# q at the edges for two quads at once, in row groups beside the first layers, in a graph attention kernel

## The chip, the core and the metric

The kernel runs on one core of a Trainium2 chip, as one launch. The metric is the device time in microseconds. The kernel before was timed in three runs, and one more execution was recorded by the hardware profiler; all stage times below are from that recorded execution.

## The reference

There are 6250 nodes with 128 features each and 206250 directed edges from a sender (`src`) to a receiver (`dst`), sorted by receiver. Cut to what matters:

```python
w   = silu(edge_feats @ rad_W1 + rad_b1) @ rad_W2 + rad_b2
w  += silu(chi_scalar @ sph_W1 + sph_b1) @ sph_W2 + sph_b2        # per edge, 32 -> 128 -> 128
q_i = (x @ Wq)[receivers];  k_j = (x @ Wk)[senders];  v_j = (x @ Wv)[senders]
alpha = (q_i * w * k_j) summed over the 16 features of each of 8 heads, / sqrt(16), * cutoffs
out = segment_sum(alpha * v_j, receivers) / 16
return layernorm(x + out)
```

All arithmetic is float32.

## The kernel before, in words

**Stages.** First the node stage: x is loaded in 13 chunks, turned on TensorE, multiplied with Wk and Wv, and the 256-wide rows of k and v are stored to a table `kv_tab` in HBM (lines 195 to 230). For the first 8 quads k and v are made directly from gathered rows of x. Then comes the edge stage, which fills nearly the whole time.

**Tiling of the edges.** 128 edges are a tile, 4 tiles are a quad (512 edges), 4 quads are a group (2048 edges): 101 groups, 403 quads. A quad's 512 edges belong to at most 32 consecutive receivers, a group's to at most 128. The edges are sorted by receiver, so q at the edges needs no gather: it is a matmul of the quad's 32 rows of q with a one-hot matrix (`hotT`, 32 x 512). The sender's k and v do need one: `gathers` (line 132) has GpSimd issue 4 indirect DMAs for each quad, 128 rows of 1 KB each, all recorded under line 114. They go to a ring of 16 quad buffers and are issued 14 quads ahead in the program.

**One quad.** `weigh` (line 382) multiplies the two hidden layers (`act`) with the second-layer weights into PSUM, and ScalarE brings it out as `w` (line 388). `take_q` (line 391) makes q at the edges in PSUM (`pq`, line 395), with features on partitions; VectorE multiplies both to `u` (line 399). `turn_back` (line 401) turns `u` with four TensorE transposes so that edges lie on partitions (`pu`, line 405). VectorE multiplies with k (`m`, line 410), sums by head (412), scales (413) and multiplies with v (`msg`, line 421). `sum_quads` (line 425) adds messages to receivers by a one-hot matmul (line 431), a group later.

**First layers.** `hidden` (line 363) makes the four first layers of a pair of quads: each has 32 contraction rows, so the four lie in the four 32-row groups of TensorE (line 372, PSUM tiles `ph`, 4 buffers, shared with `weigh` and small products), and ScalarE applies Silu (line 378). A quad j of a group has its q rows in row group j.

**Order.** The order of all engines is written out by hand. Quads are taken in slots 0 to 3 in the order j = 0, 2, 1, 3. Each slot of TensorE is: `weigh` of this quad, `turn_back` of the quad before, `take_q` of this quad, in slots 0 and 2 `hidden` for the next pair; then small products of the group: in slot 1 `sum_group` (453, 455) and `turn_q` (341), in slot 3 `make_q` (349), and parts of `sum_quads`. VectorE does `scores` of the quad before, `multiply` of this quad, `messages` of the quad before. Each gather is given a wait for a TensorE instruction of its own slot (`marks`).

**Queue of SyncE (SP).** In slot 0 it issues `load_q` (line 158): four loads, each of 32 rows of x at a row read from a table (line 119 the read, 163 the load), for the next group's `turn_q` in slot 1; then `load_xw` (128 rows of x for the layernorm) and `load_rel` (four loads that spread the edges' receiver offsets over 32 partitions each). Slot 1 has the edge features. After every fourth group `statistics` (line 464) has ScalarE change its function table, normalise four groups, and SP stores four blocks of `out` (line 486).

Of the kernel before, what the change touches and what calls it, by code (L numbers as in the profile page):

```python
# [2 lines left out]

# [18 lines left out]
WAIT = mybir.DependencyInfo(mybir.DependencyClass.Sync, mybir.DependencyReason.DATA)  # L22
# [30 lines left out]
def gnn_kernel(ctx, tc, x, src, dst, weight, edges, rad_W1, rad_b1, rad_W2, rad_b2,  # L53
# [38 lines left out]
    qb_i = const.tile([1, NG * NQ], I32, name="qb_i")  # L92
    gb_i = const.tile([1, NG], I32, name="gb_i")
    rowq = const.tile([P, NG], F32, name="rowq")
# [18 lines left out]
    def gather(o, table, index):  # L113
        return nc.gpsimd.indirect_dma_start(  # L114
            out=o, out_offset=None, in_=table,
            in_offset=bass.IndirectOffsetOnAxis(ap=index, axis=0))
# [14 lines left out]
    feats_of, relb_of, act_of, kv_of, hot_of, hotT_of, xq_of, q_of, msg_of = ({} for _ in range(9))  # L131
    po_of, part_of, to_of, tot_of, xw_of, y0_of, u_of = ({} for _ in range(7))

    def gathers(q, marks=()):

        kv = quad_of("kv", RING, 2 * D)
        for t in range(QT):
            o = gather(kv[:, t, :], kv_tab, src_i[:, q * QT + t:q * QT + t + 1])
            if marks:
                tc.add_manual_dep(o.ins, marks[t].ins.name, WAIT, reason="no gather ahead of TensorE")  # L140
        kv_of[q] = kv
# [8 lines left out]
    def load_rel(g):  # L150

        relb_of[g] = gp.tile([P, EQ], BF16, name="relb")
        for j in range(NQ):
            t = g * GT + j * QT
            nc.sync.dma_start(relb_of[g][j * W:(j + 1) * W, :],
                              rel_lin[t:t + QT, :].rearrange("t e -> (t e)").partition_broadcast(W))

    def load_q(g):

        xq_of[g] = gp.tile([P, D], F32, name="xq")  # L160
        for j in range(quads_in(g)):
            r = start_of(qb_i, g * NQ + j, N - W)
            nc.sync.dma_start(xq_of[g][j * W:(j + 1) * W, :], x[ds(r, W), :])  # L163
# [18 lines left out]
    with tc.tile_pool(name="nodes", bufs=1) as nodes, \  # L182
# [3 lines left out]
        xs_of, xT_of = {}, {}  # L186
# [7 lines left out]
        def load_x(k):  # L194
# [62 lines left out]
        def tables():  # L257
            nc.vector.tensor_scalar(gb, qb[:, :, 0], float(N - P), None, op0=OP.min)
            nc.vector.tensor_copy(qb_i, qb[:1].rearrange("p g j -> p (g j)"))
            nc.vector.tensor_copy(gb_i, gb[:1])  # L260
            load_q(0)
# [4 lines left out]
            nc.vector.tensor_scalar(rowq, rowq, roww, None, op0=OP.add)  # L266
            nc.vector.tensor_copy(rowwp, roww)
            nc.vector.tensor_copy(colp, col)
# [34 lines left out]
        for k in range(8):  # L303
            load_x(k)
            if k == 5:
                nc.sync.dma_start(dst_i, dst)
# [3 lines left out]
        for i, (k, n) in enumerate(work):  # L310
            if i + 2 < len(work):
                turn(*work[i + 2])
            kvs = k_and_v(k, n)
            for o, w in smalls[i:i + 1]:
                nc.scalar.dma_start(o, w)
            if i >= len(chunks):
                kv_of[k[0]] = kvs
                continue
            store(k, kvs)
            if k + 8 < len(chunks):  # L320
                load_x(k + 8)
# [15 lines left out]
    with tc.tile_pool(name="ps", bufs=1, space=PSUM) as pp:  # L337
        def turn_q(g):
            n = quads_in(g) * W
            pt = pp.tile([P, EQ], F32, name="ph", bufs=4)  # L340
            nc.tensor.transpose(pt[:, :n], xq_of[g][:n, :], ident[:n, :n])  # L341
            xq_of[g] = gp.tile([P, P], F32, name="xqT")
            nc.scalar.activation(xq_of[g][:, :n], pt[:, :n], AF.Copy)

        def make_q(g):

            n = quads_in(g) * W
            pt = pp.tile([P, EQ], F32, name="ph", bufs=4)
            nc.tensor.matmul(pt[:n, :D], xq_of[g][:, :n], wq, start=True, stop=True)  # L349
            q_of[g] = gp.tile([P, D], F32, name="q")  # L350
            nc.scalar.activation(q_of[g][:n, :], pt[:n, :D], AF.Copy)  # L351
# [12 lines left out]
        def hidden(pair):  # L364

            for q in pair:
                g, j = divmod(q, NQ)
                r0, c0 = 2 * R * (j // 2), EQ * (j % 2)
                for i in range(2):
                    ph = pp.tile([P, EQ], F32, name="ph", bufs=4)  # L370
                    r = slice(r0 + i * R, r0 + (i + 1) * R)
                    o = nc.tensor.matmul(ph, w1[r, :], feats_of[g][r, c0:c0 + EQ],  # L372
                                         start=True, stop=True)
                    act_of[q, i] = ph
            for q in pair:
                for i in range(2):
                    act = ep.tile([P, EQ], F32, name="act", bufs=8)
                    nc.scalar.activation(act, act_of[q, i], AF.Silu, bias=b1[:, i:i + 1])  # L378
                    act_of[q, i] = act
            return o  # L380

        def weigh(q):

            pw = pp.tile([P, EQ], F32, name="ph", bufs=4)
            for i in range(2):
                o = nc.tensor.matmul(pw, w2[:, i, :], act_of[q, i], start=(i == 0), stop=(i == 1))  # L386
            w = ep.tile([P, EQ], F32, name="w")
            nc.scalar.activation(w, pw, AF.Identity, bias=bsum)  # L388
            return w, o

        def take_q(q):
            g, j = divmod(q, NQ)
            b = slice(j * W, (j + 1) * W)
            pq = pp.tile([P, EQ], F32, name="pq")
            return pq, nc.tensor.matmul(pq, q_of[g][b, :], hotT_of[g][b, :], start=True, stop=True)  # L395

        def multiply(q, pq, w):
            u_of[q] = ep.tile([P, EQ], F32, name="u")
            nc.vector.tensor_tensor(u_of[q], pq, w, op=OP.mult)  # L399

        def turn_back(q):

            pu = pp.tile([P, QT, D], F32, name="pu")
            for t in range(QT):
                o = nc.tensor.transpose(pu[:, t, :], u_of[q][:, t * P:(t + 1) * P], ident)  # L405
            return pu, o
# [19 lines left out]
        def sum_quads(g, t, j=None):  # L426
# [3 lines left out]
            for j in range(NQ) if j is None else (j,):  # L430
                o = nc.tensor.matmul(po_of[g][j * W:(j + 1) * W, :], hot_of[g][:, j * QT + t, :],  # L431
                                     msg_of[g * NQ + j][:, t, :], start=(t == 0), stop=(t == QT - 1))
            return o
# [25 lines left out]
        def load_xw(g):  # L459
            r = start_of(gb_i, g, N - P)  # L460
            xw_of[g] = gp.tile([P, D], F32, name="xw")
            nc.sync.dma_start(xw_of[g], x[ds(r, P), :])

        def statistics(g):
# [5 lines left out]
            nc.vector.tensor_tensor(y0[:, k - 1, :], tot_of[g], xw_of[g], op=OP.add)  # L470
# [39 lines left out]

        turn_q(0)
# [5 lines left out]
        hidden(pairs[0])  # L517
        before = None
        for g in range(NG):
            last = g == NG - 1  # L520
            for slot, j in enumerate((0, 2, 1, 3)):
                q = g * NQ + j
                i = g * NQ + slot
                if q >= QUADS:
                    continue
                if slot == 0 and 2 <= g:
# [18 lines left out]
                if 1 <= g:  # L545
                    for t in ((), (0, 1), (2, 3))[slot] if last else ((), (0, 1), (2,), (3,))[slot]:
                        marks[3] = sum_quads(g - 1, t)
# [4 lines left out]
                multiply(q, pq, w)  # L552
# [3 lines left out]
                if slot == 0:  # L556
                    if g + 1 < NG:
                        load_q(g + 1)
                    if 1 <= g:
                        load_xw(g - 1)  # L560
                        if g + 1 < NG:
                            load_rel(g + 1)
                if slot == 1:
# [4 lines left out]
                    if last:  # L568
                        place(g)
                        load_xw(g)  # L570
# [9 lines left out]
        pu, _ = turn_back(before)  # L580
# [169 lines left out]
```

## Time and profile before

| what | us |
|---|---|
| median of 3 runs | 2080.5 (2072.03 to 2083.07) |
| profiled execution, own time | 2093.36 |
| its span, first to last instruction | 2091.3 |
| TensorE matmuls busy | 1919.3 |
| GpSimd busy | 1526.5 |
| VectorE busy | 1411.4 |
| ScalarE busy | 1000.9 |
| mean granted TensorE clock | 0.967 |

"Busy" is the union of an engine's instructions. Every float32 matmul of 512 columns is recorded as two passes; a busy TensorE is therefore not one at its peak. A group's row in the profile gives line, engine, operation, output<-inputs and count, then busy time and the mean duration in ns, then the idle time of the engine ahead of it and what ended that idle time ("issue": nothing that the profile shows). In the chain of work the columns are start, length and what. The granted clock is a share of full speed.

### The profile page before, as it was taken

What the parts mean: (1) busy time and instruction counts of PE and PEld (TensorE: products, weight loads), DVE (VectorE), ACT (ScalarE), POOL (GpSimd) and SP (SyncE); (2) the same over time, 40 slices, a digit from 0 to 9 for tenths busy, and PEclk for the clock granted to TensorE, in tenths of its full rate; (3) what the DMA queues carried; (4) which work ended last, traced back from release to release, by engine and by line L of the source; (5) the groups of instructions that cost most, each with busy time, mean ns of one, the idle gap of its engine ahead of it and who ended that gap; (6) DMA issues with size and microseconds to landing.
All of it is one profiled execution on the core that took longest, in us unless ns stands there. A gap on an engine that the chain in (4) does not pass through costs nothing.

```text
span 2091.3 us, 33176 instructions
## 1 busy us (share of the span) xinstructions
PE 1919.3 (92%) x9843; PEld 920.2 (44%) x9843; DVE 1411.4 (67%) x2874; ACT 1000.9 (48%) x1826; POOL 1526.5 (73%) x1620
## 2 busy tenths in 40 slices
PE   8998999989999989988998989899989999899897
PEld 7444444444444434444444444444444444444443
DVE  6676766767766766766766767667667667667666
ACT  2444545544544445444445445445445444454453
POOL 6777777777777777777777777777777777777750
PEclk9999999999999999999999999999999999999998
DMA  8545455454454454445544554554554544544540
GB/s 300 156 151 153 139 154 154 138 155 145 147 157 145 146 148 151 150 146 149 153 144 143 152 152 139 155 155 139 153 149 143 157 144 146 157 144 147 149 123 14
DMA packets 166853, 310.49 MB, mean 148 GB/s; under 512 B 46530, under 2 KB 99212, under 8 KB 166668
## 3 DMA queue, kind: packets, MB, share of 16 engines
q0 software_dynamic: 76864, 209.29, 34.3%
q1 hardware_dynamic: 88316, 98.64, 14.5%
q8 instruction: 79, 1.29, 0.2%
q14 instruction: 106, 0.87, 0.1%
q10 hardware_dynamic: 1488, 0.40, 0.1%
HBM read 294.70 MB, written 13.46 MB: 147 GB/s over the span
## 4 chain that ended last, share of the span: by engine, by line
PE 76%; ACT 9%; DMA 5%; issue 3%; SPq 3%; DVE 2%; POOL 1%; ACTq 0%; DVEq 0%
PE ph L386 32%; PE pq L395 14%; PE ph L372 11%; PE pu L405 8%; PE po L431 6%; ACT act L378 6%; DMA out<-y 2%; DMA xq<-in_x 2%; PE ph L453 2%; PE ph L349 2%; POOL msg L114 1%; SPq L163 1%; ACT y L483 1%; SPq L119 1%; PE ph L341 1%
## 5 line engine op out<-in xcount | busy, mean ns | idle before, releaser
L114 POOL DMA_INDIRECT kv<-kv_tab,src_i x1580 | 1494.8, 946 | 486.2 <-issue 261.4
L386 PE MATMUL ph<-act,w 128*128 128x512 f32 x1612 | 837.0, 644 | 78.6 <-ACT act L378 78.6
L410 DVE TENSOR_TENSOR m<-pu,kv 128x512 f32<-128x512 f32 x403 | 278.6, 691 | 557.6 <-PE pu L405 554.4
L378 ACT ACTIVATE act<-ph,b 128x512 f32<-128x512 f32 x806 | 498.5, 686 | 252.8 <-PE ph L372 239.9
L388 ACT ACTIVATE w<-ph,bsum 128x512 f32<-128x512 f32 x403 | 276.5, 686 | 456.9 <-PE ph L386 455.3
L386 PEld LDWEIGHTS ph<-act,w 128*128 128x128 f32 x1612 | 285.1, 197 | 432.4 <-issue 248.1
L395 PE MATMUL pq<-hotT,q 32*128 32x512 f32 x806 | 452.8, 641 | 0.0
L372 PE MATMUL ph<-feats,w 32*128 32x512 f32 x1612 | 398.5, 629 | 0.0
L405 PEld LDWEIGHTS pu<-ident,u 128*128 128x128 f32 x1612 | 204.1, 144 | 242.2 <-issue 155.6
L399 DVE TENSOR_TENSOR u<-pq,w 128x512 f32<-128x512 f32 x403 | 274.6, 681 | 23.7 <-ACT w L388 14.3
L412 DVE TENSOR_REDUCE side<-m 128x32 f32<-128x512 f32 x403 | 280.1, 695 | 13.7
L421 DVE TENSOR_TENSOR msg<-kv,side 128x512 f32<-128x512 f32 x403 | 272.8, 677 | 0.0
L405 PE MATMUL pu<-ident,u 128*128 128x128 f32 x1612 | 247.4, 277 | 12.7 <-DVE u L399 12.7
L372 PEld LDWEIGHTS ph<-feats,w 32*128 32x128 f32 x1612 | 158.2, 185 | 73.1 <-issue 56.1
L431 PE MATMUL po<-msg,hot 128*32 128x128 f32 x3224 | 161.4, 295 | 2.9 <-ACT part L448 2.9
L395 PEld LDWEIGHTS pq<-hotT,q 32*128 32x128 f32 x806 | 118.6, 184 | 69.7 <-issue 69.7
L431 PEld LDWEIGHTS po<-msg,hot 128*32 128x32 f32 x3224 | 75.8, 113 | 108.8 <-issue 91.3
L457 ACT ACTIVATE tot<-ph 128x128 f32<-128x128 f32 x101 | 28.0, 277 | 148.2 <-PE ph L455 139.8
L413 DVE TENSOR_TENSOR side<-side,scale 128x32 f32<-128x32 f32 x403 | 80.4, 200 | 13.8
L341 PE MATMUL ph<-ident,xq 128*128 128x128 f32 (+1 forms) x101 | 30.1, 298 | 60.8 <-DMA xq<-in_x 60.4
L351 ACT ACTIVATE q<-ph 128x128 f32<-128x128 f32 (+1 forms) x101 | 27.5, 272 | 93.1 <-PE ph L349 88.2
L360 DVE TENSOR_TENSOR hot<-rel,side 128x512 f32<-128x512 f32 x101 | 68.7, 681 | 0.0
(83 smaller groups left out, 837.2 us busy)
## 6 DMA issues: line engine op xcount, KB each, us to landing
feats<-in_edges SPq DMA_DIRECT2D x101, 512.0 KB
kv<-kv_tab,src_i POOLq DMA_INDIRECT x1580
relb<-rel_lin SPq DMA_DIRECT2D x404, 32.0 KB
xw<-in_x SPq DMA_DIRECT2D x101, 64.0 KB
out<-y SPq DMA_DIRECT2D x101, 64.0 KB
xq<-in_x SPq DMA_DIRECT2D x403, 16.0 KB
kv_tab<-kv SPq DMA_DIRECT2D x12, 512.0 KB
act<-in_x SPq DMA_DIRECT2D x12, 256.0 KB
```

What stands on the lines that cost most here:

```text
L114: return nc.gpsimd.indirect_dma_start(out=o, out_offset=None, in_=table, in_offset=bass.IndirectOffsetOnAxis(ap=index, axis=0))
L372: o = nc.tensor.matmul(ph, w1[r, :], feats_of[g][r, c0:c0 + EQ], start=True, stop=True)
L378: nc.scalar.activation(act, act_of[q, i], AF.Silu, bias=b1[:, i:i + 1])
L386: o = nc.tensor.matmul(pw, w2[:, i, :], act_of[q, i], start=(i == 0), stop=(i == 1))
L388: nc.scalar.activation(w, pw, AF.Identity, bias=bsum)
L395: return pq, nc.tensor.matmul(pq, q_of[g][b, :], hotT_of[g][b, :], start=True, stop=True)
L399: nc.vector.tensor_tensor(u_of[q], pq, w, op=OP.mult)
L405: o = nc.tensor.transpose(pu[:, t, :], u_of[q][:, t * P:(t + 1) * P], ident)
L410: nc.vector.tensor_tensor(m, pu, kv_of[q][:, :, :D], op=OP.mult)
L412: nc.vector.tensor_reduce(alpha, m.rearrange("p t (h e) -> p t h e", e=HD), AX.X, OP.add)
L421: nc.vector.tensor_tensor(msg_of[q].rearrange("p t (h e) -> p t h e", e=HD), kv_of[q][:, :, D:].rearrange("p t (h e) -> p t h e", e=HD), a ...
L431: o = nc.tensor.matmul(po_of[g][j * W:(j + 1) * W, :], hot_of[g][:, j * QT + t, :], msg_of[g * NQ + j][:, t, :], start=(t == 0), stop=(t = ...
```

## The change

**q at the edges for a pair at once.** `take_q` and `hidden` become `q_and_hidden`. In slots 0 and 2 it makes q at the edges for both quads of the present pair, and the four first layers of the next pair: the two q products use two row groups (0 and 2, or 1 and 3), the first two first layers the other two, and the last two first layers come after.

**PSUM.** `pq` and `pu`, which had one bank each, become one tile name with two banks, in turn.

**Order of TensorE.** `turn_back` of the quad before now stands ahead of `weigh` of this quad. Slots 1 and 3 have no q product any more.

**Rows of x.** `load_q` and `load_xw` become one `load_x` of the group's 128 rows, issued two groups ahead, 6 buffers. The 32-row windows of the quads are picked out of it by a matmul with a one-hot matrix `pick`, made by VectorE once a group, where a transpose stood. `off` for it is made in the node stage. `load_rel` is one load instead of four.

**Gathers.** The waits for TensorE (`marks`) go, and the issue of a slot's gathers stands at the top of the slot.

```diff
-    qb_i = const.tile([1, NG * NQ], I32, name="qb_i")
+    off = const.tile([P, NG, NQ], F32, name="off")
...
-    def gathers(q, marks=()):
+    def gathers(q):
         kv = quad_of("kv", RING, 2 * D)
         for t in range(QT):
-            o = gather(kv[:, t, :], kv_tab, src_i[:, q * QT + t:q * QT + t + 1])
-            if marks:
-                tc.add_manual_dep(o.ins, marks[t].ins.name, WAIT, reason="no gather ahead of TensorE")
+            gather(kv[:, t, :], kv_tab, src_i[:, q * QT + t:q * QT + t + 1])
...
         relb_of[g] = gp.tile([P, EQ], BF16, name="relb")
-        for j in range(NQ):
-            t = g * GT + j * QT
-            nc.sync.dma_start(relb_of[g][j * W:(j + 1) * W, :],
-                              rel_lin[t:t + QT, :].rearrange("t e -> (t e)").partition_broadcast(W))
-
-    def load_q(g):
-        xq_of[g] = gp.tile([P, D], F32, name="xq")
-        for j in range(quads_in(g)):
-            r = start_of(qb_i, g * NQ + j, N - W)
-            nc.sync.dma_start(xq_of[g][j * W:(j + 1) * W, :], x[ds(r, W), :])
+        r = rel_lin[g * GT:(g + 1) * GT, :].rearrange("(j t) e -> j (t e)", j=NQ)
+        nc.sync.dma_start(relb_of[g], r[:, None, :].to_broadcast([NQ, W, EQ]))
+
+    def load_x(g):
+        r = start_of(gb_i, g, N - P)
+        x_of[g] = gp.tile([P, D], F32, name="x", bufs=6)
+        nc.sync.dma_start(x_of[g], x[ds(r, P), :])
...
+        def pick(g):
+            n = quads_in(g)
+            pick_of[g] = gp.tile([P, NQ, W], F32, name="pick")
+            nc.vector.tensor_tensor(
+                pick_of[g][:, :n, :], colp[:, None, :W].to_broadcast([P, n, W]),
+                off[:, g, :n, None].to_broadcast([P, n, W]), op=OP.is_equal)
         def turn_q(g):
...
-            nc.tensor.transpose(pt[:, :n], xq_of[g][:n, :], ident[:n, :n])
+            nc.tensor.matmul(pt[:, :n * W], x_of[g], pick_of[g][:, :n, :], start=True, stop=True)
...
+        def q_at_edges(q):
+            g, j = divmod(q, NQ)
+            b = slice(j * W, (j + 1) * W)
+            pq_of[q] = pp.tile([P, EQ], F32, name="pq", bufs=2)
+            nc.tensor.matmul(pq_of[q], q_of[g][b, :], hotT_of[g][b, :], start=True, stop=True)
+
+        def q_and_hidden(pair, following):
+            beside = 1 - pair[0] % NQ % 2 if pair else 0
+            order = []
+            for q, n in zip_longest(pair, following):
+                if q is not None:
+                    q_at_edges(q)
+                if n is not None:
+                    order.append((n, beside))
+                    hidden_of(n, beside)
+            for n in following:
+                order.append((n, 1 - beside))
+                hidden_of(n, 1 - beside)
+            for n, i in order:
+                act = ep.tile([P, EQ], F32, name="act", bufs=8)
+                nc.scalar.activation(act, act_of[n, i], AF.Silu, bias=b1[:, i:i + 1])
+                act_of[n, i] = act
...
-            pu = pp.tile([P, QT, D], F32, name="pu")
+            pu = pp.tile([P, EQ], F32, name="pq", bufs=2).rearrange("p (t d) -> p t d", d=D)
...
+                if i + AHEAD < len(order):
+                    gathers(order[i + AHEAD])
...
-                w, mark = weigh(q)
-                marks = [mark] * QT
                 if before is not None:
-                    pu, marks[1] = turn_back(before)
-                pq, marks[2] = take_q(q)
+                    pu = turn_back(before)
+                w = weigh(q)
                 if slot % 2 == 0:
                     u = 2 * g + slot // 2 + 1
-                    if u < len(pairs):
-                        marks[3] = hidden(pairs[u])
+                    q_and_hidden(pairs[u - 1], pairs[u] if u < len(pairs) else [])
...
-                if i + AHEAD < len(order):
-                    gathers(order[i + AHEAD], marks)
...
                 if slot == 0:
+                    if g + 2 < NG:
+                        load_x(g + 2)
                     if g + 1 < NG:
-                        load_q(g + 1)
-                    if 1 <= g:
-                        load_xw(g - 1)
-                        if g + 1 < NG:
+                        pick(g + 1)
+                        if 1 <= g:
                             load_rel(g + 1)
```

`hidden_of(q, i)` issues the one first-layer matmul that `hidden` issued in its loop.

More of the change, by code (lines that the diff above doesn't have):

```diff
@@ L2 @@
 from contextlib import ExitStack
+from itertools import zip_longest
 import numpy as np
@@ L21 @@
 SP = mybir.EngineType.SP
-WAIT = mybir.DependencyInfo(mybir.DependencyClass.Sync, mybir.DependencyReason.DATA)
 P = 128
@@ L113, in gather @@
     def gather(o, table, index):
-        return nc.gpsimd.indirect_dma_start(
-            out=o, out_offset=None, in_=table,
-            in_offset=bass.IndirectOffsetOnAxis(ap=index, axis=0))
+        nc.gpsimd.indirect_dma_start(out=o, out_offset=None, in_=table,
+                                     in_offset=bass.IndirectOffsetOnAxis(ap=index, axis=0))
     def start_of(table, i, last):
@@ L130, in gnn_kernel @@
             pairs[-1].append(q)
-    feats_of, relb_of, act_of, kv_of, hot_of, hotT_of, xq_of, q_of, msg_of = ({} for _ in range(9))
-    po_of, part_of, to_of, tot_of, xw_of, y0_of, u_of = ({} for _ in range(7))
-    def gathers(q, marks=()):
+    feats_of, relb_of, act_of, kv_of, hot_of, hotT_of, x_of, q_of, msg_of = ({} for _ in range(9))
+    po_of, part_of, to_of, tot_of, xT_of, y0_of, u_of, pick_of, pq_of = ({} for _ in range(9))
+    def gathers(q):
         kv = quad_of("kv", RING, 2 * D)
         for t in range(QT):
-            o = gather(kv[:, t, :], kv_tab, src_i[:, q * QT + t:q * QT + t + 1])
-            if marks:
-                tc.add_manual_dep(o.ins, marks[t].ins.name, WAIT, reason="no gather ahead of TensorE")
+            gather(kv[:, t, :], kv_tab, src_i[:, q * QT + t:q * QT + t + 1])
         kv_of[q] = kv
@@ L185, in gnn_kernel @@
         quads_x = order[:XQ]
-        xs_of, xT_of = {}, {}
+        xs_of = {}
         smalls = []
@@ L191, in gnn_kernel, with load_nodes @@
             smalls.append((w1[i * R:(i + 1) * R, :], w))
-        def load_x(k):
+        def load_nodes(k):
             c, n = chunks[k]
@@ L258, in tables @@
             nc.vector.tensor_scalar(gb, qb[:, :, 0], float(N - P), None, op0=OP.min)
-            nc.vector.tensor_copy(qb_i, qb[:1].rearrange("p g j -> p (g j)"))
             nc.vector.tensor_copy(gb_i, gb[:1])
-            load_q(0)
+            load_x(0)
             for j in range(NQ):
@@ L266, in tables @@
             nc.vector.tensor_scalar(rowq, rowq, roww, None, op0=OP.add)
+            nc.vector.tensor_tensor(off, gb[:, :, None].to_broadcast([P, NG, NQ]), qb, op=OP.subtract)
+            nc.vector.tensor_scalar(off, off, row, None, op0=OP.add)
             nc.vector.tensor_copy(rowwp, roww)
@@ L303, in gnn_kernel @@
         for k in range(8):
-            load_x(k)
+            load_nodes(k)
             if k == 5:
@@ L320, in gnn_kernel @@
             if k + 8 < len(chunks):
-                load_x(k + 8)
+                load_nodes(k + 8)
             if k == 4:
@@ L337, in gnn_kernel @@
     with tc.tile_pool(name="ps", bufs=1, space=PSUM) as pp:
+        def pick(g):
[4 more added lines that the diff above has]
+                off[:, g, :n, None].to_broadcast([P, n, W]), op=OP.is_equal)
         def turn_q(g):
-            n = quads_in(g) * W
+            n = quads_in(g)
             pt = pp.tile([P, EQ], F32, name="ph", bufs=4)
-            nc.tensor.transpose(pt[:, :n], xq_of[g][:n, :], ident[:n, :n])
-            xq_of[g] = gp.tile([P, P], F32, name="xqT")
-            nc.scalar.activation(xq_of[g][:, :n], pt[:, :n], AF.Copy)
+            nc.tensor.matmul(pt[:, :n * W], x_of[g], pick_of[g][:, :n, :], start=True, stop=True)
+            xT_of[g] = gp.tile([P, P], F32, name="xT")
+            nc.scalar.activation(xT_of[g][:, :n * W], pt[:, :n * W], AF.Copy)
         def make_q(g):
@@ L348, in make_q @@
             pt = pp.tile([P, EQ], F32, name="ph", bufs=4)
-            nc.tensor.matmul(pt[:n, :D], xq_of[g][:, :n], wq, start=True, stop=True)
+            nc.tensor.matmul(pt[:n, :D], xT_of[g][:, :n], wq, start=True, stop=True)
             q_of[g] = gp.tile([P, D], F32, name="q")
@@ L362, in one_hots, with hidden_of @@
                 colp[:, None, :W].to_broadcast([P, GT, W]), op=OP.is_equal)
[L364 to L380, printed above, removed]
+        def hidden_of(q, i):
+            g, j = divmod(q, NQ)
+            r0, c0 = 2 * R * (j // 2) + i * R, EQ * (j % 2)
+            act_of[q, i] = pp.tile([P, EQ], F32, name="ph", bufs=4)
+            nc.tensor.matmul(act_of[q, i], w1[r0:r0 + R, :],
+                             feats_of[g][r0:r0 + R, c0:c0 + EQ], start=True, stop=True)
+        def q_at_edges(q):
+            g, j = divmod(q, NQ)
+            b = slice(j * W, (j + 1) * W)
[17 more added lines that the diff above has]
+                act_of[n, i] = act
         def weigh(q):
@@ L385, in weigh, with multiply @@
             for i in range(2):
-                o = nc.tensor.matmul(pw, w2[:, i, :], act_of[q, i], start=(i == 0), stop=(i == 1))
+                nc.tensor.matmul(pw, w2[:, i, :], act_of[q, i], start=(i == 0), stop=(i == 1))
             w = ep.tile([P, EQ], F32, name="w")
             nc.scalar.activation(w, pw, AF.Identity, bias=bsum)
[L389 to L397, printed above, removed]
+            return w
+        def multiply(q, w):
             u_of[q] = ep.tile([P, EQ], F32, name="u")
-            nc.vector.tensor_tensor(u_of[q], pq, w, op=OP.mult)
+            nc.vector.tensor_tensor(u_of[q], pq_of[q], w, op=OP.mult)
         def turn_back(q):
-            pu = pp.tile([P, QT, D], F32, name="pu")
+            pu = pp.tile([P, EQ], F32, name="pq", bufs=2).rearrange("p (t d) -> p t d", d=D)
             for t in range(QT):
-                o = nc.tensor.transpose(pu[:, t, :], u_of[q][:, t * P:(t + 1) * P], ident)
-            return pu, o
+                nc.tensor.transpose(pu[:, t, :], u_of[q][:, t * P:(t + 1) * P], ident)
+            return pu
         def scores(q, pu):
@@ L430, in sum_quads @@
             for j in range(NQ) if j is None else (j,):
-                o = nc.tensor.matmul(po_of[g][j * W:(j + 1) * W, :], hot_of[g][:, j * QT + t, :],
-                                     msg_of[g * NQ + j][:, t, :], start=(t == 0), stop=(t == QT - 1))
-            return o
+                nc.tensor.matmul(po_of[g][j * W:(j + 1) * W, :], hot_of[g][:, j * QT + t, :],
+                                 msg_of[g * NQ + j][:, t, :], start=(t == 0), stop=(t == QT - 1))
         def sum_quad(g, j):
@@ L457, in sum_group @@
             nc.scalar.activation(tot_of[g], ph[:, :D], AF.Copy)
[L459 to L462, printed above, removed]
         def statistics(g):
@@ L469, in statistics @@
             k = g - first + 1
-            nc.vector.tensor_tensor(y0[:, k - 1, :], tot_of[g], xw_of[g], op=OP.add)
+            nc.vector.tensor_tensor(y0[:, k - 1, :], tot_of[g], x_of[g], op=OP.add)
             st = gp.tile([P, 6], F32, name="st")
@@ L509, in verdict @@
             nc.vector.tensor_scalar(general, found, 0.0, None, op0=OP.is_gt)
+        pick(0)
         turn_q(0)
@@ L516, in gnn_kernel @@
         load_rel(1)
-        hidden(pairs[0])
+        load_x(1)
+        q_and_hidden([], pairs[0])
         before = None
@@ L546, in gnn_kernel @@
                     for t in ((), (0, 1), (2, 3))[slot] if last else ((), (0, 1), (2,), (3,))[slot]:
-                        marks[3] = sum_quads(g - 1, t)
-                if i + AHEAD < len(order):
-                    gathers(order[i + AHEAD], marks)
+                        sum_quads(g - 1, t)
                 if before is not None:
                     alpha = scores(before, pu)
-                multiply(q, pq, w)
+                multiply(q, w)
                 if before is not None:
@@ L569, in gnn_kernel @@
                         place(g)
-                        load_xw(g)
                 if slot == 2 and g + 1 < NG:
@@ L579, in gnn_kernel @@
         g = NG - 1
-        pu, _ = turn_back(before)
+        pu = turn_back(before)
         part_sums(g - 1)
```

## The prediction

> **What bounds the kernel now.** I read the page first, then the timeline of GpSimd, the chain of work, and the clock by stretches.
>
> The page says TensorE: 92% busy, and 76% of the chain that ended last. But one group of part 5 doesn't fit:
>
> ```profile
> PE 1919.3 (92%) x9843; PEld 920.2 (44%) x9843; DVE 1411.4 (67%) x2874; ACT 1000.9 (48%) x1826; POOL 1526.5 (73%) x1620
> ...
> L114 POOL DMA_INDIRECT kv<-kv_tab,src_i x1580 | 1494.8, 946 | 486.2 <-issue 261.4
> ```
>
> 1494.8 us of gathers and 486.2 us of idle time ahead of them are 1981 us, nearly the whole span. The timeline of GpSimd (start, length, what, idle time ahead in brackets) shows what that idle time is, at the first gathers and at the last:
>
> ```profile
> 48.33 0.94 POOL L114 DMA_INDIRECT kv<-kv_tab,src_i  x1 [5.13 <-issue]
> 49.57 0.94 POOL L114 DMA_INDIRECT kv<-kv_tab,src_i  x1 [0.30 <-issue]
> 50.82 0.95 POOL L114 DMA_INDIRECT kv<-kv_tab,src_i  x1 [0.30 <-issue]
> ...
> 2021.95 0.94 POOL L114 DMA_INDIRECT kv<-kv_tab,src_i  x1 [0.30 <-issue]
> 2023.20 0.95 POOL L114 DMA_INDIRECT kv<-kv_tab,src_i  x1 [0.31 <-issue]
> ```
>
> (2023.20 - 48.33)/1579 = 1.2507 us from gather to gather, and the first two steps are 1.24 and 1.25: GpSimd never waits, and every gather costs 0.30 us beside its 0.95. A group has 16 gathers, so GpSimd can't do a group in under 16 x 1.2507 = 20.0 us. The first 56 gathers carry no wait for TensorE and run at the same step, so the waits cost nothing.
>
> TensorE's own pace, in the chain of work (start, length, what), slots 1 and 2 of one group and the stall ahead:
>
> ```profile
> 1004.42 0.68 ACT act L378
> 1005.10 0.04 issue
> 1005.14 1.98 PE ph L386 x4
> 1007.13 0.44 PE pu L405 x4
> 1007.57 1.05 PE pq L395 x2
> ...
> 1009.94 1.92 PE ph L386 x4
> 1011.86 0.44 PE pu L405 x4
> 1012.29 0.62 PE pq L395
> 1012.91 0.41 PE ph L372 x3
> 1013.32 0.02 PE pq L395
> 1013.34 0.86 PE ph L372 x5
> ```
>
> The same place recurs at 1023.77: 18.63 us a group, 0.72 of it a wait for Silu to free a PSUM buffer of `ph`. The slot-1 q product is 1.05 us alone; the slot-2 one lies beside first layers, 0.62 + 0.41 + 0.02 + 0.86 = 1.91 together. Every fourth group is longer, 22.5 to 26.2 us by the starts of line 349:
>
> ```profile
> 976.56 7.54 SPq L486 DMA_DIRECT2D out<-y  x4
> 984.61 2.81 SPq L163 DMA_DIRECT2D xq<-in_x  x4
> ```
>
> ```profile
> 985.38:988.79 3.41, 1.12 (x6) 0.52 (x4) 2.76 (x7) 0.28 (x1) 2.67 (x3) 1.00 0.51 134
> 988.79:992.20 3.41, 3.26 (x19) 1.62 (x20) 0.00 (x0) 0.28 (x1) 2.49 (x4) 0.50 0.63 176
> ```
>
> The first block is SP's queue: four stores of `out`, each held until the store before has landed, then the loads that `turn_q` waits for. The second is stretches (length, busy TensorE, weight loads, VectorE, ScalarE, GpSimd, then granted clock, DMA share and GB/s): TensorE idles 2.3 us, and the next 3.41 us are granted half the clock. Four groups are about 3 x 18.63 + 24.1 = 80.0 us, which happens to be GpSimd's 4 x 20.0. So two nearly equal bounds run side by side. They aren't coupled: the gathers stay some 50 us ahead of their use from start to end, VectorE waits 2.2 us in all for gathered rows, and the last gather starts 68 us before the end.
>
> **The change, part by part.**
>
> *q products.* An odd slot loses 1.05 us and 0.1 for the change of row groups; the pair's products fit the 1.91 that slots 0 and 2 already pay, since there the q product of one quad heads the chain of four passes in its row group and the other three groups have room. Saved on TensorE: 202 x 1.1 = 222 us. The wait for Silu (78.6 us on 101 waits) goes too: the first layers read first now lie in row groups with no q product.
>
> *`turn_back` ahead of `weigh`.* New serial loop: turn_back 0.44, weigh to its last result 1.9, `w` 0.69, `u` 0.68, four hand-overs of 0.05: 3.9 us a slot at least. TensorE's own work: slot 0 0.44 + 1.8 + 1.91 = 4.2, slot 2 with `sum_quads` 0.36 4.5, slots 1 and 3 under 3.6. A group is 4.2 + 3.9 + 4.5 + 3.9 = 16.5; VectorE's line 355 and statistics ahead of `m` add 0.3. In every fourth group ScalarE's table loads (2 x 1.28), 0.3, 0.44 wait and 1.65 of line 483 delay `w` by about 4: mean 17.8.
>
> *Two banks.* The second q product of a pair waits for `m` to have read the turned `u` in its bank: 0.60 + 0.04 + 0.69 after turn_back starts, against 2.2 until TensorE comes there. Hidden; if `m` waits for a gather, the first layers behind it in TensorE's queue wait too, about 3 us from landing to the next turn_back, within the 5.0 that the next quad's gathers take.
>
> *`load_x`, `load_rel`.* Four loads of 0.66 to 0.9 us of SP's time and one of 0.35 become one; four of `relb` (1.8) become one. Two groups ahead is 40 us against SP's 10 us of stores, so TensorE's 60.4 us wait for `xq` and most of the half clocks after it go. At the start SP is freed by about 2.2 + 1.3 us ahead of the last `kv_tab` stores (issued at 38.5 and 39.9), whose landing frees the first gather at 48.33. GpSimd is busy until 43.2 before it, so between 0 and 4.5 us are to be had; I take 3.
>
> *`pick`, `turn_q`.* `pick` on VectorE is like line 442's 0.34: 101 x 0.34 = 34 us; VectorE needs 15 us a group of 20, so it is hidden. `turn_q` has two passes for one, 0.11 us more, in slot 1's slack. Could `pick` slow the gathers? At 58.32 one took 1.50 us beside VectorE's 1.00 us scaling of `scale`. The Trainium skill ("SBUF — State Buffer", on VectorE blocking GpSimd's descriptors) says that a VectorE operation in a two-port mode shuts GpSimd out of writing descriptors; by that rule 101 x 0.55 = 56 us, by the nearest row nothing: line 360, which like `pick` compares a PSUM and an SBUF operand, runs at 1001.07 beside gathers of 0.95. I take nothing and keep 56 as the far end.
>
> *Gather waits.* Nothing, as above.
>
> *Sum.* TensorE's path would fall to 17.8 x 101, far under GpSimd's 20.0 x 101. TensorE starts some 50 us behind the gathers and catches up by 2.2 us a group, so after about 23 groups it waits for gathers. What is saved beyond that is lost to GpSimd's step. First gather 48.3 - 3 = 45.3; last 45.3 + 1579 x 1.2507 = 2020.2; landed 2.5 later (the last packets end at 2025.7 for 2023.20). Then `m` to `msg` 2.2, statistics 2, the last sums 3.4 (2083.02 to 2086.33); SP's chain of stores, each some 2.2 behind the other, adds 0.7; from the last store to the end 4.9, as before. 2020.2 + 2.5 + 13.2 = 2036 span, own time 2038. Against 2093.4 that is 55 less.
>
> The profiled execution stood 12.9 over the median. If GpSimd's step is the same without the profiler the median is 2038; if the difference stays, 2025. I take 2032.
>
> **The rivals.**
>
> *The step is a bit shorter without the profiler.* No view can show that. If the 0.30 were 0.27, 1580 x 0.03 = 47 us less: 1990; the limit is TensorE's path, 60 + 101 x 17.8 + 10 = 1870. Against it: the packets of the gathers themselves come at that step. Chance 0.14.
>
> *The clock takes it back (slower).* Waiting for gathers, TensorE idles 5.0 - 3 us in odd slots. The Trainium skill ("TensorE: Matmul & The Clock Gate", HAM oscillation) wants no idle gap over some 3.4 us; by that nothing happens. This trace is stricter: after 2.3 us idle in the stretch above, the clock halved. Each low stretch loses 1.7 us of TensorE. From 20.0 - 17.8 = 2.2 us, that is 1.3 low stretches a group, TensorE is the bound again; at two the group is 21.2, 2091 + 101 x 1.2 = 2212. Against it: a TensorE that lags doesn't wait for gathers, idles less and keeps its clock. Chance 0.10.
>
> *`pick` slows gathers.* 2036 + 56 + 2 = 2094, less the 13: within 0.5% of 2080. Chance 0.05.
>
> *Half of it, or a longer tail, or no earlier first gather.* 2048 to 2068. Chance 0.07.
>
> **How the numbers follow.** The main case, gathers as the bound from about group 23 on, 2015 to 2048: 0.64. Range 1990 to 2062: the main case, the upper half of the first rival and most of the last. Faster 0.64 + 0.14 + 0.07 = 0.85, same 0.05, slower 0.10. (0.5%, about 10 us, is what a measurement of this kernel can tell.)
>
> **What would show it.** Gathers still 1.25 us apart over 1580; VectorE's `m` waiting for gathered rows for 150 us or more, where it was 2.2; no wait for x at `turn_q`; early groups 16.5 to 17 us with a longer fourth, later ones 20.0; last gather some 16 us before the end; mean clock under 0.967. It is wrong if gathers start under 1.25 us apart, or wait, or if groups stay over 20 us with no wait for gathers.

## The result, and the profile after

The changed kernel takes 2044.43 us (median of 4 runs, 2043.38 to 2044.89), the kernel before 2079.16 beside it (4 runs, three of them those above, 2072.03 to 2083.07): 35 us less, ratio 0.9836, 95% interval 0.9808 to 0.9864. The profiled execution of after has its own time of 2044.89 and a span of 2043.1, at a mean granted clock of 0.953. The last four runs of the study fell on two other chips, where the kernel before itself took 2521 and 2554 us; they are told at the end of the experiments and compared with nothing else.

The page of after: engines, the shares of the chain that ended last, and three groups (busy, mean ns of one, idle ahead and what ended most of it).

```profile
PE 1750.2 (86%) x9944; PEld 879.7 (43%) x9944; DVE 1448.5 (71%) x2976; ACT 966.7 (47%) x1826; POOL 1526.4 (75%) x1620
...
PE 34%; POOL 17%; DVE 16%; DMA 13%; issue 13%; ACT 6%; DVEq 0%; ACTq 0%; POOLq 0%
...
L114 POOL DMA_INDIRECT kv<-kv_tab,src_i x1580 | 1494.9, 946 | 486.7 <-issue 414.0
L421 DVE TENSOR_TENSOR m<-pq,kv 128x512 f32<-128x512 f32 x403 | 278.1, 690 | 225.3 <-DMA kv<-kv_tab,src_i 183.9
```

TensorE has lost 169 us of busy time (1919.3 before). The gathers stand as they were, 1494.9 busy and 486.7 idle ahead of them. VectorE's `m` waits 183.9 us for gathered rows. In the view of waits before (who waited for what: us in all, times, longest us) this was:

```profile
DVE m L410 <- DMA kv<-kv_tab,src_i: 2.2, 5, 0.4
```

The timeline of GpSimd, first and last gathers:

```profile
48.82 0.94 POOL L114 DMA_INDIRECT kv<-kv_tab,src_i  x1 [5.71 <-DMA scale<-in_weight]
50.07 0.95 POOL L114 DMA_INDIRECT kv<-kv_tab,src_i  x1 [0.30 <-issue]
...
2023.76 0.95 POOL L114 DMA_INDIRECT kv<-kv_tab,src_i  x1 [0.30 <-issue]
```

(2023.76 - 48.82)/1579 = 1.2508 us a step: the whole span is 48.8 ahead of the gathers, 1974.9 of gathers and 19.3 behind the last one's start. In the chain of work at mid-span, where before had a nearly unbroken row of TensorE, gathers and their landing have come in:

```profile
1033.25 0.94 POOL kv L114
1034.19 0.30 issue
...
1037.00 0.67 POOL kv L114
1037.67 0.58 issue
1038.25 3.72 DMA kv<-kv_tab,src_i
1041.97 0.03 issue
1041.99 0.05 DVEq L421
1042.05 0.04 issue
1042.09 0.70 DVE m L421
```

By the starts of the small product that makes q, ordinary early groups take 16.75 to 16.78 us and early fourth groups mostly 19.8 to 22.2. A quad's last gather starts 36.6 us ahead of its use at quad 20, 28.3 at 40, 17.3 at 60, 5.8 at 80, then mostly 3 to 6: TensorE has caught up by about group 20 (quad 80), and from there groups take 20.0 us in the mean (16.75 to 26.5 each).

### The profile page after: what moved, and what is told of

It is laid out like the page before. It is cut to its first block, busy times and chain, and to the rows that moved or that the text cites. A ratio compares the mean times of both kernels' runs of the same rounds, so it can differ in the third digit from the quotient of the medians.

```text
span 2043.1 us, 30097 instructions
## 1 busy us (share of the span) xinstructions
PE 1750.2 (86%) x9944; PEld 879.7 (43%) x9944; DVE 1448.5 (71%) x2976; ACT 966.7 (47%) x1826; POOL 1526.4 (75%) x1620
## 4 chain that ended last, share of the span: by engine, by line
PE 34%; POOL 17%; DVE 16%; DMA 13%; issue 13%; ACT 6%; DVEq 0%; ACTq 0%; POOLq 0%
PE ph L403 17%; POOL kv L114 16%; DMA kv<-kv_tab,src_i 13%; PE pq L378 6%; PE pq L416 6%; DVE u L410 5%; DVE m L421 3%; PE ph L371 3%; DVE side L423 3%; ACT w L405 3%; ACT act L396 2%; DVE msg L432 2%; POOL msg L114 1%; DVE hotT L357 1%; ACT y L488 1%
## 5 line engine op out<-in xcount | busy, mean ns | idle before, releaser
L114 POOL DMA_INDIRECT kv<-kv_tab,src_i x1580 | 1494.9, 946 | 486.7 <-issue 414.0
L403 PE MATMUL ph<-act,w 128*128 128x512 f32 x1612 | 814.6, 630 | 5.0 <-ACT act L396 4.4
L416 PE MATMUL pq<-ident,u 128*128 128x128 f32 x1612 | 271.3, 293 | 239.4 <-DVE u L410 237.3
L371 PE MATMUL ph<-feats,w 32*128 32x512 f32 x1612 | 469.9, 633 | 0.0
L421 DVE TENSOR_TENSOR m<-pq,kv 128x512 f32<-128x512 f32 x403 | 278.1, 690 | 225.3 <-DMA kv<-kv_tab,src_i 183.9
L416 PEld LDWEIGHTS pq<-ident,u 128*128 128x128 f32 x1612 | 176.7, 145 | 391.6 <-issue 218.1
L378 PE MATMUL pq<-hotT,q 32*128 32x512 f32 x806 | 291.1, 659 | 29.9 <-DVE m L421 29.4
L378 PEld LDWEIGHTS pq<-hotT,q 32*128 32x128 f32 x806 | 81.4, 190 | 233.4 <-issue 167.8
L357 DVE TENSOR_TENSOR hotT<-relb,side 128x512 f32<-128x512 bf16 x101 | 68.7, 680 | 0.0
L351 PEld LDWEIGHTS ph<-wq,xT 128*128 128x128 f32 (+1 forms) x202 | 39.1, 194 | 50.4 <-issue 49.1
L463 PEld LDWEIGHTS ph<-part,to 128*128 128x128 f32 (+1 forms) x202 | 38.5, 192 | 49.3 <-issue 29.4
```

The source lines that it names most:

```text
L114: nc.gpsimd.indirect_dma_start(out=o, out_offset=None, in_=table, in_offset=bass.IndirectOffsetOnAxis(ap=index, axis=0))
L371: nc.tensor.matmul(act_of[q, i], w1[r0:r0 + R, :], feats_of[g][r0:r0 + R, c0:c0 + EQ], start=True, stop=True)
L378: nc.tensor.matmul(pq_of[q], q_of[g][b, :], hotT_of[g][b, :], start=True, stop=True)
L421: nc.vector.tensor_tensor(m, pu, kv_of[q][:, :, :D], op=OP.mult)
```

## The experiments

Each run has the kernel before beside it on the same chip: 2093.45 us for the first four runs, 2090.52 for the next four. The changed kernel itself was not run beside them, so a difference of a few us from its 2044.43 may be one between chips.

**Half of the change at a time.** First, before with the new loads alone (one load of 128 rows two groups ahead for four of 32 rows a slot ahead, `pick`, and `relb` in one load):

```diff
-    load_q(g + 1)
-    load_xw(g - 1)
+    load_group(g + 2)      # load_x by another name
+    pick(g + 1)
...
-    nc.tensor.transpose(pt[:, :n], xq_of[g][:n, :], ident[:n, :n])
+    nc.tensor.matmul(pt[:, :n * W], x_of[g], pick_of[g][:, :n, :], start=True, stop=True)
```

> The kernel before with only the loads of x, pick and relb of the change; q products, PSUM banks, order of TensorE and the waits of gathers as before. Gathers as the floor: the wait for xq (2.4 us of each fourth group) and the half clock behind it go, four groups fall from 80.0 to about 75 to 76 us, under GpSimd's 80.0, so it ends where the changed kernel ends, about 2045 us. If the paired q products make the gain: it stays at 2070 or more.

Measured: 2044.99 us (2044.55 to 2047.6), ratio 0.9771 (0.9755 to 0.9787). Ordinary groups take 18.74 (18.62 before), and the early fourth groups 19.45, where before has 24.2 in the mean: four take 75.7, less than the gathers' 80. The lead of the gathers goes from 47.9 us at quad 20 to 3 by quad 200. Two views of this run, its page and its waits:

```profile
PE 76%; ACT 8%; DMA 6%; DVE 5%; issue 3%; POOL 0%; DVEq 0%; SPq 0%; ACTq 0%; POOLq 0%
...
L114 POOL DMA_INDIRECT kv<-kv_tab,src_i x1580 | 1498.1, 948 | 486.0 <-issue 228.9
```

```profile
DVE m L414 <- DMA kv<-kv_tab,src_i: 171.1, 88, 5.7
```

The chain says TensorE 76%, as it did before, with POOL at 0%; yet gathers set the end: line 114's 1498.1 + 486.0 nearly fills the span, and the last gather, at 2026.41, starts 19.3 us before the end, where before's starts 68 us before it. The share of the chain alone would have misled here.

Then the other half: after with the old loads, transposes and `relb`.

```diff
-    load_x(g + 2)
-    pick(g + 1)
+    load_q(g + 1)
+    load_xw(g - 1)
...
-    nc.tensor.matmul(pt[:, :n * W], x_of[g], pick_of[g][:, :n, :], start=True, stop=True)
+    nc.tensor.transpose(pt[:, :n], xq_of[g][:n, :], ident[:n, :n])
```

> The changed kernel with the old loads: four loads for q, one for the layernorm, four of relb, transposes in place of pick. Gathers as the floor: four groups are 3 x 16.8 + 16.8 + 4 to 5 for ScalarE + up to 5 for the wait for xq and the half clock, 76 to 77 us, still under 80.0, so again about 2045 us. If the loads of x make the gain: 2070 or more.

Measured: 2047.04 us (2045.64 to 2047.96), ratio 0.9783 (0.9767 to 0.9799); early ordinary groups 16.77, early fourth ones 22 to 24.5. Either half alone brings TensorE under 20.0 us a group, and either alone stops at the gathers. Whichever half is added second is worth nothing that these runs can tell.

**Without gathers.** GpSimd's four gathers of a quad are replaced by one plain load of 512 consecutive table rows, in before and in after; k and v are then wrong ones. The bytes are the same; GpSimd's busy time falls from 1526.4 to 240.1 us in after.

```diff
-        for t in range(QT):
-            gather(kv[:, t, :], kv_tab, src_i[:, q * QT + t:q * QT + t + 1])
+        r = q * EQ % ((NB - 4) * P)
+        nc.gpsimd.dma_start(kv, kv_tab[r:r + EQ, :].rearrange("(p n) d -> p n d", p=P))
```

> The kernel before with each quad's four gathers replaced by one plain load of 512 consecutive rows of the table on the same queue, with one of the four waits (so the sums use the wrong k and v; bytes and order are the same). If TensorE's path and the gathers' step are two uncoupled bounds that happen to be equal, nothing moves: 2070 to 2085 us. If the gathers held the kernel before: under 2000.

> The changed kernel with the same plain loads in place of gathers (wrong k and v). If the step of the gathers is its floor, it falls to TensorE's path as its early groups show it: 25 x (3 x 16.8 + 21.2) + 16.8 = 1807, with 58 ahead and some 20 behind about 1885 us. If half clocks and the serial loop of turn_back and weigh hold the groups at 20 us and the waits for gathered rows only mirror that: 2030 or more.

Measured, one execution each: before 2062.97 us, after 1894.2. So without gathers the change is worth 169 us; with gathers, the two halves show 46 to 49 on that chip. Groups of after take 16.75, fourth ones 21.4. In before the gathers cost 30 us though VectorE hardly waited for their rows: fourth groups are 22.7 in the mean without them and 24.2 with them, ordinary ones 18.6 either way. That is more than expected: the two bounds in the kernel before were not quite uncoupled. Which part of the fourth group's stall the gathers lengthen was not tried.

**Waits of gathers back.** In after, each gather again waits for a TensorE instruction of its own slot, and is issued behind that slot's products.

```diff
-                if i + AHEAD < len(order):
-                    gathers(order[i + AHEAD])
...
+                if i + AHEAD < len(order):
+                    gathers(order[i + AHEAD], marks)
```

> The changed kernel with each gather's wait for a TensorE instruction of its own slot back, and the gathers issued at the end of the slot as before. While TensorE trails the gathers these waits are long met; once it has caught up, gathers run 14 quads ahead in the program and still wait for work that is 65 us old. Gathers as the floor: the same time, 2044 us within 3. If the waits cost the kernel before something: 2055 or more.

Measured: 2044.88 us (2043.01 to 2046.72), ratio 0.9785 (0.9763 to 0.9806), the same as without them (2044.43 in the result).

**The start.** `relb`'s first load moved behind the last stores of the table:

```diff
-            load_rel(0)
...
             if i == len(chunks) - 1:
+                load_rel(0)
```

> The changed kernel with the first relb load moved behind the last kv_tab stores in SP's queue, where it held the queue 4.5 us (30.9 to 35.4) waiting for rel_lin to land. If that wait holds the first gather of kv, it starts 2 to 4 us earlier than 48.82 and the end moves with it, 2041 to 2042 us. If the bytes of the node stage hold it (over 300 GB/s from 38 us on): 2044.

Measured: 2041.75 us (2040.63 to 2044.51), ratio 0.9767 (0.9748 to 0.9786). GpSimd's timeline, with no idle time now between the last gather of x rows and the first of the table:

```profile
43.04 0.95 POOL L114 DMA_INDIRECT msg<-in_x,src_x  x1 [0.31 <-issue]
44.29 0.95 POOL L114 DMA_INDIRECT kv<-kv_tab,src_i  x1 [0.30 <-issue]
```

The first gather starts 4.5 us earlier. The profiled execution was the slowest of the five (2044.51): its last gather started at 2023.89, no earlier than after's, since its step was 1.2537 us where after's was 1.2508. The median is 3.1 us under that of the version with waits, which ran on the same chip, and 2.7 under after's; but the runs of the two versions on that chip overlap (up to 2044.51 here, down to 2043.01 there), so the gain is less sure than the earlier first gather.

Second, nine quads from rows of x where there were eight, so that four fewer gathers follow the table:

```diff
-XQ = 8
+XQ = 9
```

> The changed kernel with one more quad, nine for eight, whose k and v are made from gathered rows of x in the node stage: four more gathers of x run in the 5.7 us in which GpSimd idles ahead of the first gather of kv, and four gathers of kv fewer follow. Gathers as the floor: 4 x 1.25 = 5.0 us less, 2039.4 us. If the end is set by anything else: 2044, or 2046 for the added work of the node stage.

Measured: 2040.93 us (2039.17 to 2042.86), ratio 0.9763 (0.9744 to 0.9781): 3.5 us under after, and every run under those of the version with waits on the same chip. The first of the 1576 gathers starts at 48.40 and the last at 2018.75, 5.0 us earlier than after's, as forecast. Each of the two edits fills the same idle stretch of GpSimd, so I expect that they don't add up; they were not run together.

**The old order of TensorE, with no gathers.** In the kernel with plain loads (wrong k and v again), `weigh` goes back ahead of `turn_back`:

```diff
+                w = weigh(q)
                 if before is not None:
                     pu = turn_back(before)
-                w = weigh(q)
```

> As after_direct (plain loads in place of gathers, wrong k and v, 1894.2 us), with weigh ahead of turn_back again. If the serial loop turn_back, weigh, w, u sets the odd slots (3.9 us) and ScalarE's table work the fourth group, both come off the path: TensorE's own work is 15.2 us a group, plus some 0.5 us for each pair whose second q product now waits for m to free its bank: 15.2 to 16.5 a group and a fourth group within 2 of it, 1640 to 1740 us. If TensorE's work or VectorE's sets the 16.75: 1850 or more.

Measured: 1903.62 us, a clear miss of what I expected. Its waits, and a slot in its chain of work:

```profile
PEld pq L378 <- DVE m L421: 145.5, 200, 4.6
```

```profile
1004.77 0.62 PE pq L378
1005.40 0.01 PE ph L371
1005.40 0.42 PE pq L378
1005.82 0.01 PE ph L371
1005.83 0.02 issue
1005.85 0.69 PE pq L378
...
1006.97 0.86 PE ph L371 x4
```

TensorE's matmuls hardly idle (97% busy, 7.6 us of idle time ahead of the q products in all), but the weights of a pair's second q product wait for `m` to have read the transposes in its bank. The two q products then no longer overlap: their busy time is 426.7 us in the whole run, where with `turn_back` first (and no gathers) it is 231.5. The row of q products and first layers takes 3.06 us (1004.77 to 1007.83) where the prediction's lines of before show 1.91. Ordinary groups are 17.52 and fourth ones mostly 18.6, where with `turn_back` first they are 16.75 and 21.4. So the new order is what makes two shared banks enough, and the fourth groups, which ScalarE's statistics lengthen, are where it costs time; over four groups the two orders are about even (71.2 and 71.7 us).

**The end, on chips where all is slower.** The new order of the last group: a block of sums and its statistics come a slot earlier, so that ScalarE's three normalisations no longer stand between the last messages and their sum. It was run alone and with nine quads from x.

```diff
+                if last and slot == 2:
+                    part_sums(g - 1)
+                    sum_group(g - 1)
...
-        part_sums(g - 1)
+        statistics(g - 1)
```

> The changed kernel with another order in the last group alone: the layernorm of groups 96 to 98 a slot earlier, the partial sums and the total of group 99 ahead of the last turn_back, its layernorm while the last gathers are under way. In the changed kernel the last gather starts 19.3 us before the end, and the chain there runs over three y of line 488 on ScalarE, the partial sums behind them and 16 matmuls at half clock, not over the last gather. If the tail can be cut to what follows the last landed row (2.5 to landing, 2.2 to msg, some 1 for its sums, 3.4 for the last sums and y, 4.9 to the end): 14 us, so about 2039 us. If SP's chain of stores sets it: 2043 to 2044.

> Both: nine quads from gathered rows of x (measured 2040.9 us alone, gathers end 5.0 us earlier) and the new order in the last group. Gathers as the floor and a tail of 14 us: 2034 to 2036 us. If the two gains overlap: 2039.

Measured: 2873.63 us (2849.08 to 2924.61) and 2881.51 (2866.0 to 2911.7), where before took 2521.12 on that chip: ratios 1.1371 (1.1314 to 1.1428) and 1.141 (1.1377 to 1.1443). To see whether the new tail did that, the changed kernel itself and the last version were run once more, on a chip that was slow too.

> The changed kernel as it is, beside the next run on one chip. If the chip is like the first ones: 2044 us, 1.6% to 2.3% faster than before, with GpSimd stepping 1.2508 us. If the chip is like the last one, where the kernel before took 2521 us: the theory that gathers come back late there, and that the ring of 16 quads then holds GpSimd, lets both kernels be bound by the landing of gathers; then this kernel is slower than before there, by about as much as the two edits of it were (12% to 15%), and the new tail is no part of it. The rival, that the new order of the last group did that, has this kernel faster than before there.

> Nine quads from rows of x, and the new order of the last group. On a chip like the first ones: the gathers end 5.0 us earlier (four fewer), or 3.5 as measured for that edit alone (2040.9), and the tail behind the last gather shrinks from 19.3 us to about 14: 2034 to 2036 us, or 2039 if the new tail gives nothing. On a chip like the last one: within 1% of the changed kernel beside it.

Measured: 2887.63 us (2878.89 to 2924.27) for the changed kernel and 2899.5 (2867.99 to 2923.94) for the other, where before took 2553.96: ratios 1.1317 (1.1265 to 1.1369) and 1.133 (1.127 to 1.1391). So the new tail is not the cause: the changed kernel as it is loses 13% there. VectorE, ScalarE and one TensorE product in the profiled execution of the changed kernel, the longest of its six (timeline):

```profile
1023.93 0.34 DVE L453 TENSOR_SCALAR to<-side,rowp 128x128 f32<-128x128 f32 x1
1033.16 0.69 DVE L421 TENSOR_TENSOR m<-pq,kv 128x512 f32<-128x512 f32 x1 [8.88 <-remote]
```

```profile
1021.75 0.69 ACT L405 ACTIVATE w<-ph,bsum 128x512 f32<-128x512 f32 x1 [0.76 <-PE ph L403]
1026.67 0.28 ACT L467 ACTIVATE tot<-ph 128x128 f32<-128x128 f32 x1 [4.23 <-PE ph L403]
```

```profile
1021.77 0.39 PE L465 MATMUL ph<-tot,to 128*128 128x128 f32 x2
```

Such a stop of over 3.5 us ahead of `m` comes 88 times, 666 us in all; the traces of the other three runs on these two chips have 85 to 90. The theory on record, that gathers land late there, falls: a gather's last packet ends 2.42 us after its start in the median, as after's 2.43, and `m` at 1033.16 works on rows that GpSimd asked for some 105 us before. `tot` waits 4.23 us with its product done at 1022.2. "Remote" means that the trace has no releaser, and of the completions of loads only 10,476 are recorded, where after's trace has 31,252.

Two more facts narrow it down. First, the stops go with the gathers. The last gather starts at 2841.09, the last stop ends at 2825.45, and the last three groups take 16.79, 21.50 and 16.77 us, as in the kernel without gathers; the groups before them, the first aside, take 23 to 36 us. The other three traces end likewise, with groups of 16.8 to 22.2 us behind their last stops. Second, the clock adds to it: the mean granted clock is 0.81 there (0.953 in after), with 117 low stretches of 1113 us in all (42 and 196 in after). At half clock, the 917 us more would cost at most some 460 us of TensorE's time, an estimate from these sums; how much of it only follows from the stops was not separated.

What holds VectorE and ScalarE up while gathers are under way isn't shown. Why before loses less there isn't either (2521 and 2554 us, granted clock 0.88 to 0.90): there is no trace of it from such a chip, and the version with the gathers' waits back was not run there. So what the tail is worth stays unmeasured, and the cause of the loss stays open.

## Why the prediction was right, and by how much it was off

Forecast 2032 us, 1990 to 2062; measured 2044.43. The mechanism came as forecast; what was off are the two ends of the gathers, 7 us, and the guess on the difference between profiled and other runs.

**The bound** was read rightly. GpSimd's step is 1.2508 us over 1580 gathers, where 1.2507 was forecast. The medians of the two halves alone and of both together lie within 2.6 us of each other, and plain loads in the gathers' place free 150 us. "They aren't coupled" was not quite right for the kernel before: without gathers it is 30 us shorter. That did no harm, since in the changed kernel the gathers alone set the end.

**q products, `turn_back` first, two banks.** Both q products of a pair now lie beside the first layers (timeline of after):

```profile
1003.50 0.69 PE L378 MATMUL pq<-hotT,q 32*128 32x512 f32 x1
1003.51 0.69 PE L371 MATMUL ph<-feats,w 32*128 32x512 f32 x1
1003.52 0.69 PE L378 MATMUL pq<-hotT,q 32*128 32x512 f32 x1
...
1004.06 1.44 PE L371 MATMUL ph<-feats,w 32*128 32x512 f32 x5
1005.43 0.43 PE L442 MATMUL po<-msg,hot 128*32 128x128 f32 x8
```

From the first of them to the next product it is 1.93 us, where one q product and the same first layers took 1.91: the second is free, as forecast. Without gathers the q products' busy time is 231.5 us, where it was 452.8 before: 221 less (222 forecast). Groups are 16.75 us (16.5 and 0.3 forecast). Fourth groups without gathers are 21.4, 4.7 over the others (about 4 forecast), so four take 71.7, a mean of 17.9 (17.8 forecast). That the second bank is hidden holds as well, but only in the new order, as the run with the old one shows. TensorE's largest waits in after are those of the serial loop, and some of the second bank shows once `m` waits for gathered rows:

```profile
PE pq L416 <- DVE u L410: 237.3, 196, 3.5
...
DVE m L421 <- DMA kv<-kv_tab,src_i: 183.9, 115, 4.4
...
PEld pq L378 <- DVE m L421: 65.0, 51, 3.5
...
PE pq L378 <- DVE m L421: 29.4, 25, 2.7
```

TensorE's q products wait up to 3.5 us behind such an `m`, within the 5.0 that a quad's gathers take, as forecast.

**`load_x`.** TensorE's wait for `xq` before, the last number of its row,

```profile
L341 PE MATMUL ph<-ident,xq 128*128 128x128 f32 (+1 forms) x101 | 30.1, 298 | 60.8 <-DMA xq<-in_x 60.4
```

is gone; no wait for x is left at `turn_q`. The run with that half alone shows that it brings the kernel to the gathers by itself, as the other half does. The forecast that it frees the first gather failed: 48.82 instead of 45.3. The step that failed is "SP is freed by about 2.2 + 1.3 us ahead of the last `kv_tab` stores": the loads did get shorter, but SP stood at the first load of `relb`, which waits for the store of `rel_lin` to land, from 30.9 to 35.4 us (31.2 to 33.7 before), and the last stores were issued at 39.4, no earlier than the 38.5 of before. With that load moved, they were issued at 36.6, and the first gather came at 44.29. Why that wait was 2 us longer than before isn't shown.

**The last rows.** 19.3 us from the start of the last gather to the end, instead of 15.8. The sum was made from `m`, `msg`, statistics and "the last sums 3.4". The chain of after's end shows what it left out, ScalarE's part ahead of the last sums:

```profile
2026.43 1.26 ACT y L488 x3
2027.70 0.17 ACT part L458
2027.87 0.04 issue
2027.91 2.78 PE po L442 x16
2030.69 0.73 PE ph L463 x2
```

ScalarE's three normalisations of older groups end ahead of `part`, and the 16 sums behind it run at half clock (2.78 us; they follow a stretch in which TensorE was busy 0.53 of 3.40 us, and the granted clock behind it is 0.50). Both stood in the trace of before, at 2074.97 and 2076.45, and I had taken the chain up only at 2083.02. The two misses, 3.5 us each, are the 7 between the forecast span of 2036 and 2043.1.

**The difference between profiled and other runs.** I took the middle of 2025 and 2038, since the profiled execution of before stood 12.9 over the median. After's profiled execution is at its median within half a us (2044.89 and 2044.43). So the recorded step of the gathers also holds for the runs without a record. 2038 with the two misses is 2045, and taking the middle made the forecast 6 us worse. Where before's 12.9 come from isn't shown, but a rival to the profiler is on record: on the two chips of the first eight experiments before took 2088.51 to 2098.77 and 2085.43 to 2096.8 us, and 2093.36 lies in both ranges, while the kernels at the gathers' floor took 2041 to 2047 in the result and there. So the difference may be one between chips in what bounds before. The gain differs with it: 35 us in the result, 46 to 50 there.

**The rivals.** A step that is shorter without the profiler: excluded by that same agreement. `pick` slowing the gathers: the step of 1.2508 with 101 of them in it leaves no room for 56 us; the prediction had not shown that `pick` is a two-port operation, of which that rule speaks. The clock: low stretches did grow, from 28 (142 us) to 42 (196 us), in stretches like these (length, busy TensorE, weight loads, VectorE, ScalarE, GpSimd, clock, DMA share and GB/s):

```profile
917.40:920.80 3.40, 0.56 (x5) 0.59 (x6) 2.88 (x6) 0.00 (x0) 2.49 (x4) 1.00 0.41 125
920.80:924.20 3.40, 3.40 (x9) 0.86 (x7) 1.91 (x5) 0.00 (x0) 2.75 (x3) 0.50 0.42 123
```

It cost nothing ahead of the last rows: the gathers keep their step and stay ahead of their use. That fits the reason given against it, that a TensorE that lags stops waiting for gathers; group times after the catch-up swing between 16.75 and 26.5 us around the gathers' 20.0. The rule of the Trainium skill ("TensorE: Matmul & The Clock Gate", HAM oscillation), no idle gap over some 3.4 us, was too mild here as well. TensorE has 18 such gaps in after, of 3.5 us, against 42 low stretches; the first stretch above has 2.84 us of idle time, and the stretches ahead of the 42 have 0.9 to 3.4.

## What to carry to other kernels

Add up busy time and the idle time ahead of a group that repeats at a constant step: where the two fill the span, that engine is a floor, whatever its busy share and its share of the chain say, and work taken from another engine pays only down to it. How far before the end the group stops tells whether the kernel is already at it (68 us here before the change, 19 after). When two parts of a change each reach the floor, test them one at a time; here either was enough. A forecast at a floor is as good as its two ends: follow the chain of the end from the last bound instruction on, not from the last sums.

## What the runs showed that was not expected

- A gather's mean step differs between executions: 1.2508 us in one and 1.2537 in another, 0.2%, or 4.6 us of this kernel. Behind the first eighth of the gathers, each eighth of the one has 1.2499 to 1.2513, of the other 1.2530 to 1.2537.
- A product can be fully paid for while the matmuls hardly idle: with the old order TensorE was busy 97% of the time and still no faster, since the row of a pair's q products and first layers took 3.06 us instead of 1.93.
- On two chips where before took 2521 to 2554 us, the change made the kernel 13% slower, with stops of VectorE and ScalarE that end when the gathers end. The sign of a change can depend on the chip, so a comparison needs both kernels on the same one.
